# Regrouping the columns of a sparse matrix inside on-chip memory, in a graph layer followed by a mixture of experts

## The chip, the cores and the metric

The kernel runs on one core of a Trainium2 chip. The metric is device time in microseconds (us) of one execution. A core has five engines that run their own instruction streams and wait for each other by semaphores: TensorE (PE; its weight loads are PEld), VectorE (DVE), ScalarE (ACT), GpSimd (POOL) and SyncE (SP), which here only issues transfers. The transfers themselves are done by 16 DMA engines. On-chip memory (SBUF) has 128 rows, called partitions; matrix products land in a smaller memory, psum.

## The reference

A graph layer and a mixture of experts, one after the other, each with a residual:

```python
# x [2048, 256], src/dst [67584] with dst sorted, edge_weight [67584], node_vec1 [2048, 1]
xn = layernorm(x)
out = segment_sum(edge_weight[:, None] * xn[dst], src, 2048)   # edge_index = stack([src, dst])
x = x + out + node_vec1

xn = layernorm(x)
logits = xn @ Wr + br                  # 8 experts
top_p, top_idx = top_k(softmax(logits), 2)
weights = top_p / top_p.sum(-1)
for e in range(8):                     # hidden size 1024, exact gelu
    y[e] = gelu((layernorm(xn) * ln_g[e] + ln_b[e]) @ W1[e] + b1[e]) @ W2[e] + b2[e]
x = x + sum_k weights[:, k] * y[top_idx[:, k]]
```

The graph layer is a product A xn with a 2048 x 2048 matrix A that has an entry for each pair (src, dst) with edges, the sum of their weights.

## The kernel before

**Edge part.** The kernel makes A dense, block by block, and multiplies. A has 16 column blocks (a block is 128 values of dst) and 16 row blocks. The edges are sorted by dst, so two neighbouring columns ("a group") own a short window of edges. For each half of a column block (32 groups, 64 columns) `make_hots` (line 299) builds one-hot matrices of the edges: `hl` (line 306, VectorE) says which row within a row block, `eq` (line 311, VectorE) which row block and which of the two columns, and `hr` (line 318) is `eq` times the weight, split in three bfloat16 parts (two by VectorE, the third by GpSimd). `make_cols(n, ...)` (line 329) multiplies them on TensorE (line 343): 96 small products for a half block, n = 0 to 31, four groups at once in the four quarters of the array. The result in psum, `pa`, has 128 rows (4 groups x 2 columns x 16 row blocks, that is 8 columns of A times 16 row blocks) and, for four such m, 128 values each (the rows within a block). ScalarE copies it to `ar` (line 346, two copies for a half block; `ar` has three buffers).

The dense product wants a column of A in one partition: `ac` is [128 columns, 16 row blocks, 128]. So the 8 x 16 rows of `ar` have to become 8 rows with 16 pieces of 512 bytes each. Before the change this goes by way of memory: line 347 writes a half block to `ad` in memory (SP's queue, 512 KB), and after the second half line 350 reads the whole block back as `ac` (SP's queue, 1024 KB).

`dense(cbs, b)` (line 352) multiplies `ac` of a list of column blocks with the normalised rows `xn_sb` for two row blocks (line 357), and `add` (line 361) adds the result to `acc` on VectorE (lines 364 and 367). The column blocks come in groups of 3, 3, 3, 3 and 4 (`CS`, line 73); a group has 8 calls of `dense`, one for each pair of row blocks. `ac` tiles are in two rings, `cols_1` and `cols_0`, that the groups use in turn, with four buffers each; so a block of group g + 2 takes a buffer of group g, once that group's 8 calls are done.

The order is written by hand (manual schedule): step n issues the one-hots of n + 1, the additions of the calls of the step before, `make_cols(n)`, and then as many calls of `dense` as a budget allows (lines 500 to 507). The budget grows by 3.5 column blocks a step from n = 8 on; a call on three column blocks costs 3. In the last step, n = 31, all that is left of the first four groups is issued. The last group's calls follow after the branch at line 569, which is for inputs that the windows don't cover and isn't taken.

**Routing and experts.** The last group's calls alternate with the squares, the layer norm, the logits and the choice of two experts (lines 1088 to 1104). Rows are then sorted into slots of 256 of one expert, and each slot runs two layers on TensorE (lines 1013 and 1027). The weights of the first experts are asked for by SP (lines 932 to 935) right behind the last columns. SP's queue also carries, within the edge part, two blank blocks (lines 547 and 549) and small tables (line 540).

Of the kernel before, what the change touches and what calls it, by code (L numbers as in the profile page):

```python
# [9 lines left out]
F32 = mybir.dt.float32  # L10
# [11 lines left out]
P = 128  # L22
# [4 lines left out]
def kernel(  # L27
# [30 lines left out]
    nc = tc.nc  # L58
# [3 lines left out]
    NB = N // P  # L62
# [3 lines left out]
    GC = 2  # L66
# [3 lines left out]
    GB = P // GC  # L70
    GH = GB // 2
    QP = P // RK
# [15 lines left out]
    dram = ctx.enter_context(tc.tile_pool(name="dram", bufs=1, space=DRAM))  # L88
# [89 lines left out]
    pool_of = {cb: (cols_1, cols_0)[g % 2] for g, cbs in enumerate(groups) for cb in cbs}  # L178
# [150 lines left out]
    def make_cols(n, hl, hr):  # L329


        cb, h = n // 2, n % 2
        if h == 0:
            ads[cb] = dram.tile([P, NB, P], F32, name="ad", bufs=4)
        ad_v = ads[cb].rearrange("(m j) b r -> (j b) m r", m=GB // QP)
        ar = rowsp.tile([P, GH // QP, P], F32, name="ar")
        for m0 in range(0, GH // QP, 4):
            pa = ps_a.tile([P, 4, P], F32, name="pa")
            for m in range(4):
                for i in range(3):  # L340
                    for j in range(QP):
                        g = (m0 + m) * QP + j
                        nc.tensor.matmul(pa[j * RK:(j + 1) * RK, m, :], hr[:, i, g, :],  # L343
                                         hl[:, g, :], start=(i == 0), stop=(i == 2),
                                         tile_position=(0, j * RK))
            nc.scalar.copy(ar[:, m0:m0 + 4, :], pa)  # L346
        nc.sync.dma_start(ad_v[:, h * GH // QP:(h + 1) * GH // QP, :], ar)
        if h == 1:
            acs[cb] = pool_of[cb].tile([P, NB, P], F32, name="ac")
            nc.sync.dma_start(acs[cb], ads[cb])  # L350

    def dense(cbs, b):

# [14 lines left out]
                                           acc[:, b + i, :D], op0=OP.add, op1=OP.add)  # L368
        nc.vector.tensor_add(acc[:, b:b + 2, D:], acc[:, b:b + 2, D:], pa[:, :, D:DX])

    ads, acs = {}, {}
    ET = mybir.EngineType
    ALL = {ET.DVE, ET.Pool, ET.PE, ET.Activation, ET.SP}
    with tc.manual_schedule(engines=ALL):
# [88 lines left out]
        for n in range(NH):  # L463
# [3 lines left out]
            m = n % 4  # L467
# [26 lines left out]
            for p in late:  # L494
                add(*p)
            late = []
            make_cols(n, *hots.pop(n))


            if n >= 8:  # L500
                budget += 3.5
            while len(todo) > NB // 2 and (budget >= len(todo[0][0]) or n == NH - 1):
                cbs, b = todo.pop(0)
# [17 lines left out]
            if n == 1:  # L521
# [5 lines left out]
                for rows in (b1_rows, g_rows, be_rows, nv_rows):  # L527
                    m = rows.shape[0]
# [40 lines left out]
    with tc.If(n_used < E):  # L569
# [11 lines left out]
        with tc.tile_pool(name="any", bufs=2) as anyp, tc.tile_pool(  # L581
            name="ps_any", bufs=2, space=PSUM
# [594 lines left out]
    with tc.manual_schedule(engines=ALL - {ET.Pool}):  # L1177
        for q in range(4):
            r = slice(q * N // 4, (q + 1) * N // 4)
# [33 lines left out]
```

## Time and profile before

| | us |
|---|---|
| median of three runs | 506.23 |
| lowest and highest of them | 504.37, 507.13 |
| the profiled execution | 508.05 |
| its span, first to last instruction | 506.3 |
| TensorE busy | 459.8 (91%) |
| VectorE busy | 273.1 (54%) |
| GpSimd busy | 192.7 (38%) |
| ScalarE busy | 183.8 (36%) |

The profile's page gives, for one execution, the busy time of each engine, a picture of it in 40 slices, the DMA queues, the chain of work that ended last, the costliest groups of instructions, and the transfers by line with the median time from issue to landing. A group's line reads: source line, engine, operation, destination <- sources, count | busy us, mean ns of one | idle time of the engine before them and what ended most of it. A float32 product of the dense part appears as two records of its matmul. Other views of the same trace give the instructions in order of time, the waits, and the busy time of each engine in any stretch, with the clock that TensorE was granted (1.00 is full speed), the share of the DMA engines' time and GB/s.

### The profile page before, as it was taken

Reading aid. Unit: us, or ns where it says so; the run is one execution under the profiler, and the core shown is the slowest. Engines: PE = TensorE matmul, PEld = TensorE weight load, DVE = VectorE, ACT = ScalarE, POOL = GpSimd, SP = SyncE. Lnnn points to the kernel's source line nnn. Section 1 sums busy time; section 2 is a strip of 40 time slices with the busy share of each in tenths; the row PEclk is TensorE's granted clock in tenths of the full one; section 3 lists DMA queues with packets and bytes.
Section 4 is the critical chain, followed back from the end, with each engine's and each line's share of the span. In section 5 each row is a group of like instructions: output and inputs, shape, how many; then the busy total and the mean of one; then the engine's idle time right before and its main releaser. Section 6 shows DMA issues by size and latency. Waiting matters only on the chain.

```text
span 506.3 us, 12113 instructions
## 1 busy us (share of the span) xinstructions
PE 459.8 (91%) x4996; PEld 394.4 (78%) x4996; DVE 273.1 (54%) x621; ACT 183.8 (36%) x422; POOL 192.7 (38%) x158
## 2 busy tenths in 40 slices
PE   4876599898979999899999899999999999999993
PEld 3775478687758878788888788888888888888882
DVE  7999999999969971317837232323232312212111
ACT  2478524144214210028483323332243433333320
POOL 3477655544533330000142444443452444322231
PEclk9575679899979999999999999999999999999998
DMA  6128678796777667953513997997999677226420
GB/s 214 53 76 246 203 223 269 230 236 186 203 216 221 210 178 239 344 189 105 179 54 84 303 333 214 361 356 210 334 360 309 169 210 210 36 40 204 140 92 31
DMA packets 84356, 102.15 MB, mean 202 GB/s; under 512 B 8240, under 2 KB 74656, under 8 KB 82176
## 3 DMA queue, kind: packets, MB, share of 16 engines
q1 hardware_dynamic: 74832, 86.26, 53.5%
q0 software_dynamic: 7984, 13.91, 11.9%
q10 hardware_dynamic: 1472, 1.06, 0.7%
q8 instruction: 44, 0.72, 0.6%
q14 instruction: 24, 0.20, 0.1%
HBM read 75.18 MB, written 28.14 MB: 204 GB/s over the span
## 4 chain that ended last, share of the span: by engine, by line
PE 35%; DMA 13%; issue 3%; DVE 1%; SPq 0%; ACT 0%; POOL 0%; POOLq 0%; DVEq 0%
PE py L1027 16%; PE ph L1013 15%; DMA xs<-xr_d,to_i 8%; DMA y_d<-ys,to_i 2%; DMA out<-y_d 2%; PE px L978 1%; PE px L834 1%; PE py L357 1%; DMA so_far<-out,to_i 1%; DMA out<-ys,to_i 0%; SPq L1180 0%; POOL out L1048 0%; POOLq L1209 0%; ACT L1015 0%; DVE pick L957 0%
## 5 line engine op out<-in xcount | busy, mean ns | idle before, releaser
L357 PE MATMUL py<-xn_sb,ac 128*128 128x264 f32 x512 | 126.3, 404 | 1.8 <-DVEq L569 1.4
L1013 PE MATMUL ph<-xeT,w 128*128 128x256 f32 (+1 forms) x576 | 121.3, 368 | 2.4 <-PEq L1167 1.7
L1027 PE MATMUL py<-w,hT 128*128 128x256 f32 x544 | 121.0, 379 | 0.0
L1013 PEld LDWEIGHTS ph<-xeT,w 128*128 128x128 f32 x576 | 104.4, 190 | 16.5 <-issue 3.0
L357 PEld LDWEIGHTS py<-xn_sb,ac 128*128 128x128 f32 x512 | 98.5, 197 | 21.7 <-issue 2.2
L1027 PEld LDWEIGHTS py<-w,hT 128*128 128x128 f32 x544 | 101.9, 190 | 12.9
L1015 ACT ACTIVATE hT<-ph,ec 128x256 f32<-128x256 f32 (+1 forms) x144 | 66.2, 462 | 117.6 <-PE ph L1013 60.8
L1035 POOL DMA_INDIRECT y_d<-ys,to_i x30 | 48.5, 1616 | 119.3 <-DVE ys L1030 88.5
L318 POOL TENSOR_TENSOR hr<-eq,w 128x1024 bf16<-128x1024 bf16 x32 | 61.2, 1912 | 81.6 <-DVE hr L318 66.1
L343 PE MATMUL pa<-hl,hr 128*32 128x128 bf16 x3072 | 58.4, 237 | 21.6 <-POOL hr L318 10.8
L343 PEld LDWEIGHTS <-hr 128*32 128x32 bf16 x3072 | 50.0, 106 | 32.6 <-issue 14.0
L306 DVE TENSOR_TENSOR hl<-k,iota_t 128x4096 bf16<-128x4096 bf16 x32 | 72.9, 2278 | 0.0
L987 DVE TENSOR_SCALAR xeT<-px,ec 128x256 f32<-128x256 f32 (+1 forms) x38 | 18.4, 526 | 79.8 <-PE px L978 79.0
L939 POOL DMA_INDIRECT xs<-xr_d,to_i x39 | 40.5, 1038 | 54.2 <-DVE z L702 41.9
L346 ACT COPY ar<-pa 128x512 f32<-128x512 f32 x64 | 36.5, 584 | 59.8 <-PE pa L343 53.6
L1030 DVE SCALAR_TENSOR_TENSOR ys<-py,wt,b2w 128x256 f32<-128x256 f32 x34 | 16.4, 484 | 72.7 <-PE py L1027 61.3
L364 DVE TENSOR_TENSOR acc<-acc,py 128x528 f32<-128x528 f32 x32 | 22.3, 701 | 35.3 <-PE py L357 35.3
L318 DVE TENSOR_TENSOR hr<-eq,w 128x2048 bf16<-128x2048 bf16 x32 | 39.1, 1223 | 0.6
L1002 ACT ACTIVATE b2w<-b,wt 128x256 f32<-128x256 f32 x36 | 16.3, 500 | 34.0 <-DVE wt L1000 32.4
L311 DVE TENSOR_TENSOR eq<-k,iota_t 128x1024 bf16<-128x1024 bf16 x32 | 21.8, 680 | 0.0
L670 ACT ACTIVATE sq<-acc,less_m 128x256 f32<-128x256 f32 x16 | 8.0, 499 | 32.6 <-DVE acc L364 32.6
L296 ACT CAST w<-r 128x256 bf16<-128x256 f32 x16 | 6.5, 405 | 25.0 <-DVE r L295 25.0
(196 smaller groups left out, 303.0 us busy)
## 6 DMA issues: line engine op xcount, KB each, us to landing
w<-in_L_ffn_W SPq DMA_DIRECT2D x40, 1024.0 KB, 9.2
ad<-ar SPq DMA_DIRECT2D x32, 512.0 KB, 8.7
ac<-ad SPq DMA_DIRECT2D x16, 1024.0 KB, 5.9
b<-in_L_ffn_b SPq DMA_DIRECT2D x20, 128.0 KB, 9.8
out<-y_d SPq DMA_DIRECT2D x4, 512.0 KB, 6.3
xr_d<-rec SPq DMA_DIRECT2D x1, 1300.0 KB
y_d<-acc SPq DMA_DIRECT2D x1, 1280.0 KB, 5.1
acc<-in_x SPq DMA_DIRECT2D x2, 512.0 KB, 7.6
```

The source lines that it names most:

```text
L306: nc.vector.tensor_tensor(hl.rearrange("p g (n t) -> p g n t", t=2), two(k2[:, 0], g, P), pair(P), OP.is_equal)
L311: nc.vector.tensor_tensor(eq.rearrange("p g (n t) -> p g n t", t=2), two(k2[:, 1], g, RK), pair(RK), OP.is_equal)
L318: return engine.tensor_tensor(hr[:, i0:i1].rearrange("p i g (n t) -> p (i g) n t", t=2), eq[:, None, :, :].to_broadcast([P, i1 - i0, GH, RK]),
L343: nc.tensor.matmul(pa[j * RK:(j + 1) * RK, m, :], hr[:, i, g, :], hl[:, g, :], start=(i == 0), stop=(i == 2), tile_position=(0, j * RK))
L346: nc.scalar.copy(ar[:, m0:m0 + 4, :], pa)
L357: nc.tensor.matmul(pa[:, i, :DX], acs[c][:, b + i, :], xn_sb[:, c, :], start=(c == cbs[0]), stop=(c == cbs[-1]))
L364: nc.vector.tensor_add(acc[:, b:b + 2, :], acc[:, b:b + 2, :], pa[:, :, :DX])
L939: nc.gpsimd.indirect_dma_start(out=(sets[s.set][0] if into is None else into)[:, t, :], out_offset=None, in_=(xr_d if rows is None else ro ...
L1013: nc.tensor.matmul(ph, w1[:, k, c * P:(c + 1) * P], xeT[:, k, :], start=(k == 0), stop=(k == KD - 1))
L1015: nc.scalar.activation(hT[:, c, :s.n * P], ph, AF.Gelu, bias=ec[:, c:c + 1], scale=1.0)
L1027: nc.tensor.matmul(py, hT[:, c, t * P:(t + 1) * P], w2[:, c, :], start=(c == 0), stop=(c == KH - 1))
L1035: st = nc.gpsimd.indirect_dma_start(out=y_d[:, :], out_offset=bass.IndirectOffsetOnAxis(ap=tos[s.to][:, t:t + 1], axis=0), in_=ys, in_offs ...
```

## The change

`make_cols` no longer goes by way of memory. The tile `ac` is claimed in the first half of a column block instead of after the second, and behind each copy of line 346 SP issues four transfers of 64 KB, each from one m of `ar` (128 rows of 512 bytes) to 8 rows of `ac` (16 x 512 bytes each): 8 for a half block, 256 in all. The memory tile `ad` is gone. The budget of dense products grows from n = 7 on.

```diff
         cb, h = n // 2, n % 2
         if h == 0:
-            ads[cb] = dram.tile([P, NB, P], F32, name="ad", bufs=4)
-        ad_v = ads[cb].rearrange("(m j) b r -> (j b) m r", m=GB // QP)
+            acs[cb] = pool_of[cb].tile([P, NB, P], F32, name="ac")
         ar = rowsp.tile([P, GH // QP, P], F32, name="ar")
         for m0 in range(0, GH // QP, 4):
             pa = ps_a.tile([P, 4, P], F32, name="pa")
...
             nc.scalar.copy(ar[:, m0:m0 + 4, :], pa)
-        nc.sync.dma_start(ad_v[:, h * GH // QP:(h + 1) * GH // QP, :], ar)
-        if h == 1:
-            acs[cb] = pool_of[cb].tile([P, NB, P], F32, name="ac")
-            nc.sync.dma_start(acs[cb], ads[cb])
+            for m in range(m0, m0 + 4):
+                c = (h * GH // QP + m) * QP * GC
+                nc.sync.dma_start(acs[cb][c:c + QP * GC], ar[:, m, :])
...
-            if n >= 8:
+            if n >= 7:
                 budget += 3.5
```

More of the change, by code (lines that the diff above doesn't have):

```diff
@@ L369, in add @@
         nc.vector.tensor_add(acc[:, b:b + 2, D:], acc[:, b:b + 2, D:], pa[:, :, D:DX])
-    ads, acs = {}, {}
+    acs = {}
     ET = mybir.EngineType
```

## The prediction

> **What bounds the kernel now.** I read the page first. TensorE is busy for 459.8 us of 506.3, and the chain that ended last begins at 229.95 us and is mostly TensorE's own work, so whatever moves the end of the edge part moves the end of the kernel. Then I took the instructions in order of time around the end of the edge part, the starts of the one-hots (line 306), and the DMA queue's own waits.
>
> ```profile
> L357 PE MATMUL py<-xn_sb,ac 128*128 128x264 f32 x512 | 126.3, 404 | 1.8 <-DVEq L569 1.4
> ad<-ar SPq DMA_DIRECT2D x32, 512.0 KB, 8.7
> ac<-ad SPq DMA_DIRECT2D x16, 1024.0 KB, 5.9
> ```
>
> The first line (group, busy us, mean ns, idle before) says that the dense products are 512 records, and that none but 1.8 us of idle TensorE stands before them: the columns come late for nobody, and the trip through memory (8.7 us and then 5.9 us to landing) is hidden for 15 of the 16 column blocks. The last one is hidden too:
>
> ```profile
> 188.34 0.29 PE L343 MATMUL pa<-hl,hr 128*32 128x128 bf16 x8
> 190.42 1.41 PE L343 MATMUL pa<-hl,hr 128*32 128x128 bf16 x88 [1.78 <-POOLq L569]
> 191.26 1.21 ACT L346 COPY ar<-pa 128x512 f32<-128x512 f32 x2 [5.12 <-PE pa L343]
> 191.76 16.29 PE L357 MATMUL py<-xn_sb,ac 128*128 128x264 f32 x72
> ...
> 198.34 0.33 SPq L350 DMA_DIRECT2D ac<-ad  x1
> ...
> 209.45 25.16 PE L357 MATMUL py<-xn_sb,ac 128*128 128x264 f32 x112 [1.40 <-DVEq L569]
> ```
>
> Columns: start, duration, engine, line, records, idle time before and its releaser. The last half block's products end at 191.8 us. TensorE then works off what is left of the dense products, 72 records in 16.29 us, to 208.05 us. In that time the last columns land (198.34 + 5.9 = 204.2 us), 3.8 us before TensorE is free. So the path here is the backlog of dense products, not the columns. One call of dense() on three column blocks is 12 records, 12 x 16.29 / 72 = 2.72 us.
>
> ```profile
> 74.00:184.00 110.00, 102.88 (x2220) 83.67 (x2220) 99.99 (x129) 35.49 (x84) 48.11 (x30) 0.95 0.75 219
> L306 DVE TENSOR_TENSOR hl<-k,iota_t x32: 2253/2279/2286, 18.2 to 184.2; 128x4096 bf16<-128x4096 bf16 x32
> ```
>
> The stretch 74 to 184 us (busy us of TensorE, weight load, VectorE, ScalarE, GpSimd; granted clock, DMA share, GB/s) has TensorE at 94% and VectorE at 91%: two engines nearly full. The 32 one-hots start from 18.2 to 184.2 us, so a half block takes 166.0 / 31 = 5.35 us. That is the beat that the new transfers must keep.
>
> **The change, part by part.** *Dense one half block sooner.* The budget of 3.5 per half block starts at n = 7. The trace has 512 - 72 - 128 = 312 records before the backlog, 26 calls; with one more step the budget reaches 28 of the 32 calls, and the order of the built program shows that 4 are left after the last half block. The backlog shrinks from 72 records to 48, by 24 x 0.226 = 5.43 us. The two calls go elsewhere. One goes to n = 7, where TensorE waits for GpSimd's third factor twice (1.68 us before 59.83, 1.30 us before 63.88): 2.98 us of idle cover its 2.72 us, so it costs 0; without that cover 2.7 us. The first call today also waits for its columns (4 records at 66.35, the other 8 from 68.88 us); that could give back up to 1.8 us, of which I count nothing, since VectorE's beat comes next. The other call makes n = 30 a double one, ahead of the last half block, where TensorE today idles 1.78 us before 190.42: it costs 2.72 - 1.78 = 0.94 us. Its add on VectorE (0.70 us) falls into VectorE's 5.22 us of idle after 189.5 us, cost 0. Sum: -5.43 + 0.94 = **-4.5 us**.
>
> *The way through memory.* Removed: 32 transfers to memory and 16 back, and the wait of each second one for the first (102.9 us of waiting in SP's queue, which held up only later transfers). Added: 256 transfers of 64 KB (8 rows of 16 x 512 bytes), four behind each copy of line 346. Three things must each keep the beat, 5.35 / 8 = 0.67 us per transfer.
>
> ```profile
> L1180 SPq DMA_DIRECT2D out<-y_d x4: 576/594/1129, 474.8 to 477.3; - x4
> L350 SPq DMA_DIRECT2D ac<-ad x16: 332/333/338, 41.8 to 198.3; - x16
> 194.00:195.00 1.00, 1.00 (x7) 0.84 (x6) 0.26 (x1) 0.00 (x0) 0.00 (x0) 1.00 1.15 348
> ```
>
> (i) SP's issue: between 0.333 us and, in a row of four issued back to back, 0.594 us median and 1.129 us at most. I take 0.594 (the row of transfers issued back to back): 8 x 0.594 = 4.75 us of 5.35, it just fits. (ii) In flight: the built program has each transfer wait for the one eight places before it. Landings in the trace run from 4.0 us (8 KB, be_rows) to 8.7 us (512 KB); eight per landing is 0.50 to 1.09 us each. I take 4.0, since 64 KB is nearer to 8 KB than to 512: it fits. (iii) The movement itself. At 194 us only a transfer out of ar, in the same 512-byte pieces, is on the move: 348 GB/s with all 16 engines, or 0.19 us for 64 KB. If only as many engines work as there are destination rows, 8 of 16, it is 0.38 us. At the other end, if the rate goes with the rows written (348 GB/s over 128 rows, 2.7 GB/s a row), 8 rows take 21.75 GB/s, 3.0 us. No transfer in this trace writes so few rows with so many bytes. I take 0.38 us, from the row with the same source and the same pieces: 3.0 us of 5.35, hidden behind the one-hots.
>
> [...]
>
> New waits. The column tile is now claimed in the first half of its block instead of at the end, so its buffer must be free a half block sooner; dense() runs a half block sooner as well, and the program's order keeps only two transfers that wait for TensorE, where seven did (2.5 us of waiting in all). Behind such a one stand SP's next column transfers, and behind those ScalarE's copies once the three ar buffers are full, that is after two half blocks, 10.7 us: cost 0, and at most one call of 2.7 us if that cover is gone. ScalarE's copy into a reused ar waits for eight semaphores instead of one; today it waited for ad<-ar 5.3 us in three places, none of which TensorE's path shows, so 0. The small tables (line 540) hold SP's next transfer for 5.05 us today; that happens once more, behind the same three buffers: 0.
>
> The end of the edge part, now: TensorE's last products end near 192.7 us (191.76 + 0.94), the backlog of 4 calls takes 10.9 us, to 203.6. The last copy ends at 192.5 + 0.6; four issues (2.4 us) and the landing (6.3 us, out<-y_d, as a high value) give 201.8 us. So the columns are in 1.8 us before they are needed. The weights of the first expert follow on SP some 3 us sooner and land behind the columns; they are not read before 248 us. The 1.40 us at the branch (line 569) stays and is next, then the last group's products, all moved up together.
>
> Gaps of TensorE that no semaphore explains (0.42, 1.76, 1.44, 0.32, 3.06 us at 89 to 145 us) may shrink with less DMA traffic or grow with worse; I count 0, with 4 us to either side.
>
> Sum: 508.05 (profiled execution: span 506.3 and 1.75 around it) - 4.5 = 503.5. That execution lies 1.8 us over the median of the three runs, 506.23; against the median I predict **501.7 us** (506.23 - 4.5), by itself 497 to 503.5.
>
> **Rivals.** *A, few rows make it slow (slower than before).* The movement costs more than 0.67 us a transfer: from there on it sets the beat, ScalarE's copies wait for ar, TensorE for ScalarE's psum. With the middle (geometric) of 0.38 and 3.0, 1.07 us: 31.0 (first issue) + 256 x 1.07 + 6 (landing) = 311 us, against 209.45 for the start of the last group, so +101 us: 608 us. For it: 8 rows at a time, where every large transfer in the trace uses 128. Against it: four transfers behind one another go to different rows, and engines that run ahead of each other could use them at once; the DMA share of 0.75 falls, as half the bytes go. The outer end, 3.0 us, would be 31 + 768 + 6, +596 us, near 1,100.
>
> *B, the queue sets the beat.* Issue or the eight in flight take more than 0.67 us a transfer. With the 6.3 us landing of out<-y_d: 6.4 / 8 = 0.80 us, 31 + 205 + 6 = 242 us, +32: 539 us. For it: 0.594 leaves 11% of room, and VectorE's short steps (4.7 us) leave none. Against it: the early and the double steps are longer, and three ar buffers even it out.
>
> *C, nothing to gain.* The columns were hidden before and TensorE at 94% just does the calls elsewhere: what the backlog loses, the edge part gains, and only the idle found at n = 30 and n = 7 remains, 2 us or less, perhaps lost to a longer clock drop (the granted clock is 0.5 at 144 to 149 us already). 505 us. The change would then do what it says and not matter.
>
> **How the numbers follow.** 0.5% of 506.2 is 2.5 us, about what a measurement of this kernel can tell from no change. Forecast (hidden, backlog shorter): 0.40. A: 0.33, a quarter of it above 640. B: 0.15. C: 0.12, of which 0.10 within 0.5% and 0.02 slower. Faster 0.40, same 0.10, slower 0.50: the likeliest single case is the fast one, though the slow ones together outweigh it. The range runs from 498 (under it 0.05) to 640, which takes in B, the middle of A and most of what lies above it; left out are 0.08 above and the outer end of the movement's price.
>
> **What will show it.** Right: 48 records of line 357 (the dense products) in one block after the last half block, no wait of ScalarE's copies for the transfers, one-hots still at 5.35 us a half block, the last group starting near 204 us. A: copies that wait for the column transfers in each half block, one-hots 8 us or more apart, TensorE's granted clock no excuse. B: SP's queue full of issues, or waiting for the transfer eight before, with little DMA share. C: the steps at n = 7 and n = 30 longer by a call. What would make it wrong above all is step (iii), the price of writing 64 KB into 8 rows.

## The result, and the profile after

The changed kernel takes 525.11 us (median of four executions, 515.78 to 532.27) against 506.68 us of the kernel before (504.37 to 508.92). The ratio is 1.0285, with a 95% interval of 1.0215 to 1.0354: slower, where 501.7 us was predicted. The ratio and its interval leave out executions more than 1.5% above the fastest of their kernel (here 527.25 and 532.27 us), the medians do not. The profiled execution is the fastest of the four: 515.78 us, span 513.8, that is 7.5 us over the span of before. The execution profiled before is one of its longer ones (508.05 us, where the median of the 35 recorded in all is 504.64), so 7.5 us is rather too little. The trace below explains most of these 7.5 us and not the rest of the spread.

On the page of the changed kernel, the group of dense products, the copy to `ar` (line 345 now), and the transfers:

```profile
L355 PE MATMUL py<-xn_sb,ac 128*128 128x264 f32 x512 | 129.0, 408 | 7.3 <-DMA ec<-cols_d 4.2
L345 ACT COPY ar<-pa 128x512 f32<-128x512 f32 x64 | 35.3, 586 | 79.2 <-DMA ac<-ar 60.3
ac<-ar SPq DMA_DIRECT2D x256, 64.0 KB
```

TensorE now stands idle for 7.3 us ahead of the dense products; it was 1.8 before the change. The second line is the new one: ScalarE waits 60.3 us for column transfers, because all three `ar` buffers are still being read. A wait of ScalarE alone need cost nothing (before the change it stood 59.8 us ahead of the same copies); the instructions of SP's queue in order of time (start, duration, line, count) show what lies behind it:

```profile
29.59 51.12 SPq L348 DMA_DIRECT2D ac<-ar  x72
80.82 0.43 SPq L545 DMA_DIRECT2D xr_d<-none  x1
81.29 0.46 SPq L547 DMA_DIRECT2D y_d<-none  x1
81.85 21.64 SPq L348 DMA_DIRECT2D ac<-ar  x32
103.60 0.41 SPq L538 DMA_DIRECT2D cols_d<-by_e  x1
104.10 106.86 SPq L348 DMA_DIRECT2D ac<-ar  x152
213.16 0.37 SPq L930 DMA_DIRECT2D ec<-cols_d  x1
```

From 29.6 to 211 us SP issues column transfers almost without a pause; three other transfers stand between them. The tile view of `ac` gives the durations of the 256 issues (min, median, max in ns) and the starts of the first and the last:

```profile
L348 SPq DMA_DIRECT2D ac<-ar x256: 604/613/1441, 29.6 to 210.3; - x128
```

From one start to the next it is (210.3 - 29.6) / 255 = 0.709 us on average. In the undisturbed stretches it is 0.672 (eight transfers in 5.38 us; 0.613 of issue and 0.059 until the next one starts), and no eight take less. The other 9.4 us (255 x 0.037) are a dozen stretched issues of up to 1.44 us (5.0 us over the usual ones), the three other transfers (1.7 us), one wait for ScalarE's copy near 36 us (1.4 us) and small gaps. The beat allows 0.669. The difference, 0.040 x 255, is 10.2 us, and by so much the last column transfers come late. At 0.672 alone it would be 0.8 us: the issue takes all the room that the beat has, and whatever comes on top is never made up. TensorE, in order of time at the two ends of the edge part:

```profile
63.07 2.13 PE L355 MATMUL py<-xn_sb,ac 128*128 128x264 f32 x4
66.44 3.86 PE L355 MATMUL py<-xn_sb,ac 128*128 128x264 f32 x8 [1.24 <-DMA ac<-ar]
...
196.36 10.95 PE L355 MATMUL py<-xn_sb,ac 128*128 128x264 f32 x48
208.70 1.57 PE L355 MATMUL py<-xn_sb,ac 128*128 128x264 f32 x6 [1.40 <-DMA ac<-ar]
214.52 26.22 PE L355 MATMUL py<-xn_sb,ac 128*128 128x264 f32 x106 [4.24 <-DMA ec<-cols_d]
```

The backlog has the 48 records that were forecast, but it starts at 196.36, not 192.7, and then the last columns are missing: after six records TensorE stands 4.24 us and goes on at 214.52. Before the change the seventh record of this group came at 210.8 us (209.45 + 6 x 25.16 / 112), so that is 3.7 us late. The name ec<-cols_d there is that of the transfer issued right behind the columns; the packet records have the last 512-byte piece of a column at 213.4 us, just before TensorE goes on.

The rest of the group is slower as well: 106 records in 26.22 us, where 106 took 23.8 us at the pace of before. The granted clock is the last figure but two in these windows, of the kernel before and of the changed one:

```profile
209.00:235.00 26.00, 25.43 (x120) 21.50 (x121) 8.97 (x27) 10.41 (x32) 0.00 (x0) 1.00 0.66 224
```

```profile
214.00:241.00 27.00, 26.22 (x106) 21.73 (x106) 7.83 (x23) 10.27 (x31) 0.00 (x0) 0.90 0.88 297
```

So 6.1 of the 7.5 us are there at the end of this block: 3.7 of standing and 2.4 of slower products at a granted clock of 0.90 instead of 1.00.

### The profile page after: what moved, and what is told of

The parts are those of the page before. It is cut to its first block, busy times and chain, and to the rows that moved or that the text cites. A ratio compares the mean times of both kernels' runs of the same rounds, so it can differ in the third digit from the quotient of the medians.

```text
span 513.8 us, 12518 instructions
## 1 busy us (share of the span) xinstructions
PE 467.0 (91%) x4996; PEld 396.9 (77%) x4996; DVE 273.0 (53%) x621; ACT 182.5 (36%) x422; POOL 192.8 (38%) x158
## 4 chain that ended last, share of the span: by engine, by line
PE 38%; DMA 13%; issue 4%; DVE 1%; ACT 1%; SPq 0%; POOL 0%; POOLq 0%; DVEq 0%; ACTq 0%
PE py L1025 16%; PE ph L1011 15%; DMA xs<-xr_d,to_i 7%; PE py L355 4%; DMA y_d<-ys,to_i 2%; DMA w<-in_L_ffn_W 2%; DMA out<-y_d 1%; PE px L976 1%; PE px L832 1%; DMA so_far<-out,to_i 1%; DMA out<-ys,to_i 0%; SPq L1178 0%; POOL out L1046 0%; DMA ec<-cols_d 0%; DVE acc L362 0%
## 5 line engine op out<-in xcount | busy, mean ns | idle before, releaser
L355 PE MATMUL py<-xn_sb,ac 128*128 128x264 f32 x512 | 129.0, 408 | 7.3 <-DMA ec<-cols_d 4.2
L1011 PE MATMUL ph<-xeT,w 128*128 128x256 f32 (+1 forms) x576 | 123.0, 372 | 2.7 <-PEq L1165 2.0
L1011 PEld LDWEIGHTS ph<-xeT,w 128*128 128x128 f32 x576 | 105.5, 192 | 17.5 <-issue 3.3
L342 PE MATMUL pa<-hl,hr 128*32 128x128 bf16 x3072 | 59.5, 233 | 18.3 <-POOL hr L318 10.6
L345 ACT COPY ar<-pa 128x512 f32<-128x512 f32 x64 | 35.3, 586 | 79.2 <-DMA ac<-ar 60.3
L408 PEld LDWEIGHTS pa<-wc,ar 128*128 128x128 f32 x64 | 11.2, 272 | 3.5 <-ACT ar L402 3.1
```

Source lines behind the costliest of these rows:

```text
L355: nc.tensor.matmul(pa[:, i, :DX], acs[c][:, b + i, :], xn_sb[:, c, :], start=(c == cbs[0]), stop=(c == cbs[-1]))
L1011: nc.tensor.matmul(ph, w1[:, k, c * P:(c + 1) * P], xeT[:, k, :], start=(k == 0), stop=(k == KD - 1))
```

## The experiments

**Theory T**: the number of issues is the price. SP cannot issue column transfers closer than 0.672 us on average, and that is the beat's whole allowance. **Rival M** (later **P**): moving 64 KB into 8 rows is the price. **Rival F**: the eight transfers in flight are. Line numbers in the fences are those of each kernel, a few off from the changed one.

### Issue from two engines

```diff
-                nc.sync.dma_start(acs[cb][c:c + QP * GC], ar[:, m, :])
+                (nc.sync, nc.scalar)[m % 2].dma_start(acs[cb][c:c + QP * GC], ar[:, m, :])
```

> The same 256 transfers, issued in turn by SP and by ScalarE. Theory (SP's issue sets the beat: 0.672 us from one issue to the next, 5.38 us for the eight of a half block, and 12.7 us behind ScalarE's last copy at the end): SP has 128 issues, 2.7 us a half block, the last columns land near 197 us, TensorE does not wait for them, time 499 to 504 us. Rival M (moving 64 KB into 8 rows sets the beat, issue only waits behind it): the movement is the same, last columns near 210 us, time 514 to 526. Rival F (eight in flight sets the beat): as M, since the eight are shared.

Measured: 563.67 us (558.34 to 575.46), ratio 1.1113 (1.0968 to 1.1258). T's number is missed by 60 us. ScalarE's waits, by line (total us, times, longest):

```profile
ACT ar L345 <- DMA ac<-ar: 55.0, 20, 5.5
ACT w L296 <- DMA ac<-ar: 14.8, 6, 3.6
ACT k L281 <- DMA ac<-ar: 12.2, 5, 4.1
```

With the issues on ScalarE's own stream its other work (lines 296 and 281, which feed VectorE's one-hots) stands behind transfers too. And one transfer still takes 0.88 us on average (256 from 30.4 to 253.8), though two queues issue: with half of the issues taken from SP, something else sets the spacing. SP now waits for it, 60.5 us for the transfer eight before against 0.3 us in the changed kernel. The packet records point at the movement: a 512-byte piece takes 60 ns on average here (30 to 255 us), 43 in the changed kernel (30 to 212 us). Why it is slower from two queues is not shown. So T is not the whole of it: taking half of the issues from SP brought nothing here (ratio 1.1113, where the changed kernel has 1.0285). They went to an engine with work of its own, at 0.624 us each (median; 0.613 on SP).

### The same number of transfers, into all rows

```diff
-                c = (h * GH // QP + m) * QP * GC
-                nc.sync.dma_start(acs[cb][c:c + QP * GC], ar[:, m, :])
+                nc.sync.dma_start(acs[cb][:, h * GH // QP + m, :], ar[:, m, :])
```

and the same bytes in a quarter of the transfers:

```diff
+            u = h * GH // QP + m0
+            nc.sync.dma_start(acs[cb][:, u:u + 4, :], ar[:, m0:m0 + 4, :])
```

> 256 transfers of 64 KB from SP as in the changed kernel, in the same 512-byte pieces, but each into all 128 rows of the column tile (one piece a row) instead of 8 rows; the columns then stand in the wrong places, so the graph layer multiplies with another matrix of the same shape. Theory (issue): nothing gets better, issues 0.67 us apart, last columns near 210 us, 512 to 525 us; only the issues that are stretched beyond 0.61 us may go (7 us in all, at most). Rival M: the movement falls to some 0.2 us a transfer, SP is no longer held, and the time falls to 500 to 504 us.

> As rows_128 (columns in the wrong places), but the four transfers behind a copy are one of 256 KB: the same bytes and pieces in 64 issues instead of 256. Theory (issue): SP has two issues a half block, the last columns land within 4 us of the last copy, 499 to 504 us. Rival M: no difference to rows_128. Rival F: faster than rows_128 as well, since fewer are in flight; the spacing of the issues in rows_128 tells it from the theory.

Measured: 545.01 us (541.6 to 546.84) and 522.52 us (520.41 to 523.77). The columns lie in wrong places, the routing differs and more expert slots run (5146 matmuls instead of 4996 in the first), so only the edge part is compared. The issues, and TensorE at the end of the edge part, first of the 256 transfers, then of the 64:

```profile
L347 SPq DMA_DIRECT2D ac<-ar x256: 464/599/1985, 30.1 to 223.0; - x128
```

```profile
204.94 10.95 PE L354 MATMUL py<-xn_sb,ac 128*128 128x264 f32 x48
217.30 7.36 PE L354 MATMUL py<-xn_sb,ac 128*128 128x264 f32 x32 [1.41 <-DVEq L566]
```

```profile
186.20 10.95 PE L354 MATMUL py<-xn_sb,ac 128*128 128x264 f32 x48
198.54 25.16 PE L354 MATMUL py<-xn_sb,ac 128*128 128x264 f32 x112 [1.39 <-DVEq L566]
```

Into 128 rows 256 transfers are no faster than into 8 (0.756 us from start to start, last group at 217.30), although they move fast: a 512-byte piece takes 27 ns, and SP never waits for the transfer eight before. T had expected 0.67 us and fewer stretched issues, and missed that: 27 of them cost 23 us over the usual issue, where the changed kernel has a dozen and 5.0 us. A quarter of the issues, with the same bytes and the same 512-byte pieces, brings the last group to 198.54, 18.8 us sooner and 10.9 sooner than the kernel before (the shorter backlog is in the 10.9). That is T: where nothing but the number of issues, and with it the size of each, changes, the delay goes. M is refuted as the cause of the floor, and F with it.

### The way on chip alone

```diff
-            if n >= 7:
+            if n >= 8:
```

> The on-chip transfers alone, dense products from n = 8 as before. Theory (issue): the last columns still land near 213 us; the longer backlog (72 records, 16.3 us) ends near 211, so it fills time in which TensorE waits in the changed kernel: the same as the changed kernel within 3 us, 513 to 526. If the second part did cost something by itself (a longer step at n = 7 and n = 30, buffers claimed too soon), this is faster than the changed kernel by 3 us or more; if buffers of the column tiles hold SP back, it is slower by 3 us or more.

Measured: 530.48 us (519.9 to 543.36), over the 513 to 526 expected, and profiled in its longest execution, so the total tells nothing finer than "as slow as both parts together". SP also waits 5.6 us there for column buffers that TensorE still reads (nothing in the changed kernel); what that costs cannot be told from this spread. The windows of the long execution (TensorE, weight load, VectorE, ScalarE, GpSimd busy; clock, DMA share, GB/s):

```profile
74.00:150.00 76.00, 68.15 (x1453) 54.94 (x1455) 67.01 (x96) 23.56 (x61) 35.77 (x24) 0.96 0.57 117
158.00:190.00 32.00, 24.13 (x497) 19.08 (x496) 25.28 (x24) 4.90 (x10) 10.19 (x6) 0.95 0.65 71
```

From 158 us on the DMA engines are busier and move less: 71 GB/s at a share of 0.65, 109 GB/s to a full share, against 205 before that. There the issues still take 0.613 us, but SP waits between them and eight transfers take 7.7 us instead of 5.38, 0.96 us each. The clock is no excuse (0.96 and 0.95). That is M's mechanism, in part of the time. That it is what makes this execution longer than others is not shown, since no shorter one of this kernel was profiled.

### The order of the rows

All eight transfers of a half block behind its second copy, once so that neighbours in the queue go to rows 32 apart, once in plain order (range(8) in place of the list) as a control:

```diff
-            for m in range(m0, m0 + 4):
-                c = (h * GH // QP + m) * QP * GC
-                nc.sync.dma_start(acs[cb][c:c + QP * GC], ar[:, m, :])
+        for m in (0, 4, 1, 5, 2, 6, 3, 7):
+            c = (h * GH // QP + m) * QP * GC
+            nc.sync.dma_start(acs[cb][c:c + QP * GC], ar[:, m, :])
```

Rival P takes the place of the rows for the price: with neighbours 32 rows apart, a transfer should cost 0.97 us or more in all of the edge part (the author's estimate; 0.96 was measured in the slow stretch of chip_from_8).

> All eight transfers of a half block are issued behind its second copy, in the order m = 0, 4, 1, 5, 2, 6, 3, 7, so that neighbours in the queue go to rows 32 apart (rows 0-7, then 32-39, then 8-15 and so on). The same is computed. Theory T (SP's issue, 0.672 us from one transfer to the next, is the floor, and where the rows lie does not matter): 0.67 us a transfer as in the changed kernel, last group at 214 to 218 us, total 515 to 532. [...]

> The control of same_ports: all eight transfers behind the second copy, but in the order m = 0 to 7, as the changed kernel has them. The same is computed. Both theories: like the changed kernel, 0.67 us a transfer in most stretches, last group 214 to 218 us, total 515 to 532 (1 to 2 us more at the end, as the last eight wait for the second copy). If this one is as slow as same_ports, the order of the rows says nothing.

Measured: 532.18 us (527.96 to 535.32), ratio 1.0505 (1.0441 to 1.0570), against 517.09 (514.39 to 519.6), ratio 1.0243 (1.0193 to 1.0292) for the control. SP's column transfers and its waits for the transfer eight before, rows 32 apart first:

```profile
30.08 69.58 SPq L348 DMA_DIRECT2D ac<-ar  x72
...
124.25 107.70 SPq L348 DMA_DIRECT2D ac<-ar  x152
```

```profile
SPq L348 <- DMA ac<-ar: 18.3, 34, 1.4
```

and the control:

```profile
30.23 52.22 SPq L348 DMA_DIRECT2D ac<-ar  x72
...
106.12 106.91 SPq L348 DMA_DIRECT2D ac<-ar  x152
```

```profile
SPq L348 <- DMA ac<-ar: 1.3, 3, 0.7
```

The order of the rows costs 15 us, with the same issues of the same bytes: place matters, and T's "where the rows lie does not matter" is wrong. But it costs only in the first 72 transfers (0.97 us each against 0.73); the last 152 take the same time in both, so P's 0.97 us in all of the edge part is wrong as well. Within the 72 it goes higher, rows 32 apart first, then the control:

```profile
43.92 21.36 SPq L348 DMA_DIRECT2D ac<-ar  x19
```

```profile
43.81 21.47 SPq L348 DMA_DIRECT2D ac<-ar  x32
```

In the same time 19 transfers go out instead of 32, 1.12 us each against 0.67. Two limits lie side by side: the issue, 0.67 us at best for transfers into 8 rows; and the movement, which is usually hidden behind it and in some stretches takes 0.96 to 1.16 us (1.16 for the slowest sixteen in a row here). Why rows 32 apart are the slower order, and why a stretch of slow movement begins and ends, is open.

### The dense products sooner, without the transfers on chip

The way through memory, budget from n = 7:

```diff
-            if n >= 8:
+            if n >= 7:
                 budget += 3.5
```

> The way through memory of the kernel before, and the dense products one half block sooner. The same is computed. If the second part of the change is worth what the prediction gave it (backlog 72 to 48 records, -5.4 us, n = 30 +0.9): 501.7, ratio 0.991. Theory T: the gain is real only where the columns are there; the call at n = 7 waits for column block 2, which through memory lands near 69 us, so TensorE stands still for some 3 to 5 us more there and gives most of it back: 504 to 507, ratio 0.997 to 1.002.

Measured: 507.21 us (505.68 to 509.18), before 505.39, ratio 1.0036 (1.0010 to 1.0061). TensorE at n = 7 and behind the last half block:

```profile
62.78 2.13 PE L357 MATMUL py<-xn_sb,ac 128*128 128x264 f32 x4
69.76 3.75 PE L357 MATMUL py<-xn_sb,ac 128*128 128x264 f32 x8 [4.85 <-DMA ac<-ad]
...
196.23 12.56 PE L357 MATMUL py<-xn_sb,ac 128*128 128x264 f32 x48 [2.28 <-issue]
210.19 25.16 PE L357 MATMUL py<-xn_sb,ac 128*128 128x264 f32 x112 [1.40 <-DVEq L569]
```

The call stands 4.85 us for column block 2, as T had it, and there is no gain (if anything, 0.4% slower). That the one makes the other is not shown by this trace: the last half block's products end near 194 us, only 1 us later than in the next kernel, and 3.9 us more go at the backlog, in an idle that no semaphore explains (2.28) and in slower records (12.56 us instead of 10.95; the granted clock is 0.91 from 192 to 210 us). With a larger step instead of an earlier start, as many calls leave the backlog, and the first comes at n = 8 as in the kernel before:

```diff
             if n >= 8:
-                budget += 3.5
+                budget += 3.75
```

> The kernel before with a budget of 3.75 instead of 3.5 column blocks a step from n = 8: the columns go through memory, no call comes before its columns, and two calls more are done before the last half block, as in the changed kernel (backlog 48 records). The same is computed. T: 72 to 48 records is -5.4 us, +0.9 at the end, last group near 204 to 206, total 501 to 503, ratio 0.991 to 0.995. V: the last half block's products come 3 us or more later than 190.4, last group at 207 to 210, ratio 0.998 to 1.004.

Measured: 503.05 us (499.54 to 507.59), before 504.64, ratio 0.9943 (0.9906 to 0.9981): faster than both kernels, than the one before by little.

```profile
65.27 1.16 PE L357 MATMUL py<-xn_sb,ac 128*128 128x264 f32 x4
70.50 3.46 PE L357 MATMUL py<-xn_sb,ac 128*128 128x264 f32 x8 [4.08 <-DMA ac<-ad]
...
191.73 1.41 PE L343 MATMUL pa<-hl,hr 128*32 128x128 bf16 x88 [0.55 <-POOLq L569]
193.08 10.95 PE L357 MATMUL py<-xn_sb,ac 128*128 128x264 f32 x48
205.42 25.16 PE L357 MATMUL py<-xn_sb,ac 128*128 128x264 f32 x112 [1.40 <-DVEq L569]
```

In this execution the first call waits as well, 4.08 us, and yet the time is made up by the end of the edge part, which speaks further against the wait at n = 7 as the whole cause above. The last half block's products come 1.3 us later than before (190.42), the backlog has 48 records, the last group starts 4.0 us sooner. So in this form the shorter backlog is worth something: -2.9 us measured (504.64 x 0.0057; by the interval -1.0 to -4.7), where -4.5 us was forecast for the form with the earlier start.

### A few blocks on chip

Column blocks 2 and 15 on chip, the others through memory, budget from n = 7; then blocks 0, 1, 2 and 15; `(2, 15)` becomes `(0, 1, 2, 15)`:

```diff
-            acs[cb] = pool_of[cb].tile([P, NB, P], F32, name="ac")
+            if cb in (2, 15):
+                acs[cb] = pool_of[cb].tile([P, NB, P], F32, name="ac")
+            else:
+                ads[cb] = dram.tile([P, NB, P], F32, name="ad", bufs=4)
...
+        if cb in (2, 15):
+            return
+        ad_v = ads[cb].rearrange("(m j) b r -> (j b) m r", m=GB // QP)
+        nc.sync.dma_start(ad_v[:, h * GH // QP:(h + 1) * GH // QP, :], ar)
...
```

> Only column blocks 2 and 15 go by transfers on chip (32 instead of 256), the other 14 through memory; dense products one half block sooner. The same is computed. Theory T (the issues cost, not the way itself): a burst of 16 transfers per block, 0.67 us each, is 10.8 us in 10.7 us of two half blocks and leaves no queue behind; the call at n = 7 has its columns in time, the last columns land near 200 us, before the backlog of 48 records ends: last group near 204 to 206, total 501 to 504, ratio 0.990 to 0.996. Rival P (movement into few rows sets the beat everywhere): 32 transfers at 0.97 us or more, 15.5 us per block, the columns of block 2 some 5 us late and those of block 15 near 205: 505 to 509, ratio 0.998 to 1.005.

> Column blocks 0, 1, 2 and 15 go by transfers on chip (64 in all), the other 12 through memory; dense products one half block sooner. The same is computed. In two_blocks the first call at n = 7 stood 6.0 us for column block 2, whose transfers sat in SP's queue behind the read of block 1. Theory T (the issues are the price; the second part of the change is worth its 4.5 us where the columns are there): the first call waits 1.3 us or less, the last group starts near 204 to 206, total 501 to 504, ratio 0.991 to 0.997. Rival V (VectorE sets the pace of the edge part at 98% from 74 to 130 us, the calls done sooner push the end of the edge part back by what they take off the backlog): one-hots end at 186 us or later, last group at 207 to 210, 505 to 508, ratio 0.998 to 1.004.

Measured: 506.75 us (503.33 to 511.78), before 505.39, ratio 1.0025 (0.9987 to 1.0063); and 505.33 us (502.24 to 513.8), before 504.64, ratio 1.0004 (0.9969 to 1.0040). Both miss T's totals and lie in those of the rivals, P (505 to 509) and V (505 to 508). TensorE at n = 7 and at the last group, first with two blocks, then with four:

```profile
61.81 1.16 PE L366 MATMUL py<-xn_sb,ac 128*128 128x264 f32 x4
68.95 3.56 PE L366 MATMUL py<-xn_sb,ac 128*128 128x264 f32 x8 [5.98 <-DMA ad<-ar]
...
208.09 25.16 PE L366 MATMUL py<-xn_sb,ac 128*128 128x264 f32 x112 [1.40 <-DMA w<-in_L_ffn_W]
```

```profile
66.67 1.66 PE L366 MATMUL py<-xn_sb,ac 128*128 128x264 f32 x4
69.11 2.02 PE L366 MATMUL py<-xn_sb,ac 128*128 128x264 f32 x8 [0.78 <-DMA ac<-ar]
...
205.50 25.16 PE L366 MATMUL py<-xn_sb,ac 128*128 128x264 f32 x112 [1.40 <-DVEq L578]
```

With two blocks, block 2 comes no sooner than through memory: SP issues its first transfer at 52.7 us, after the read of block 1, and the 16 take 13.0 us, between T's 10.8 and P's 15.5. With four, the wait is 0.78 us and the last group starts at 205.50, as T said and not V (207 to 210); that profiled execution, 502.24 us, is the fastest of its twelve, and the others take it back. What they spend it on was not traced: inconclusive, and V is not refuted for them.

Two more, built on rate_375's edit with block 15 alone on chip, the second with a step of 4:

> As rate_375, with column block 15 alone on chip (16 transfers). The same is computed. Through memory the last columns land near 204 us, just when a backlog of 48 records ends; on chip a copy at 192 us and 8 issues of 0.67 us with a landing of 2 to 3 us give 200 to 201. T: equal to rate_375 or up to 1 us better, ratio 0.989 to 0.995. V: 0.998 to 1.004.

> A budget of 4 column blocks a step from n = 8 (backlog 24 records), with column block 15 alone on chip. The same is computed. T: another 2 calls out of the backlog, 5.4 us, against 2 x 2.9 us of TensorE's time in an edge part with 6.9 us of idle from 74 to 184 us, of which rate_375 uses most: equal to rate_375_last within 2 us, and the columns of block 15 then come just as the backlog ends; ratio 0.988 to 0.997. V: slower, the end of the edge part pushed back by more than the backlog loses, ratio 1.000 to 1.010.

Measured: 503.37 us (500.81 to 511.32), ratio 0.9972 (0.9942 to 1.0003), not to be told from rate_375 and not from the kernel before; and 506.45 (502.39 to 509.68), ratio 1.0014 (0.9977 to 1.0051). With the step of 4 only 24 records are left, and the columns are late: TensorE stands 5.78 us in the last group and goes on with its seventh record at 209.63, only 1.2 us sooner than before (210.8). The movement shows here too: the last eight of the 16 transfers start 0.93 us apart, the first eight 0.69. More out of the backlog than the columns' landing allows is not a gain.

## Why the prediction was wrong, point by point

- **Step (i), SP's issue, failed.** It took 0.594 us for an issue and compared 8 x 0.594 = 4.75 us with a beat of 5.35. Measured: 0.613 us of issue, 0.059 to the next, and 0.037 for stretched issues and what else stands in the queue, 0.709 on average, 5.67 us for eight. The duration was 3% off; the error was to take a duration where the beat needs the time from start to start. The row quoted for it had that time too: four issues from 474.8 to 477.3 us are 2.5 / 3 = 0.83 us apart. With that number the step would not have fit. It is rival B's mechanism, priced there at 0.80 us and 539 us, measured at 0.709 and 525. The prediction named step (iii) as the one that would make it wrong; it was this one. Rows_128_four, where the same bytes go in a quarter of the issues, shows it.
- **Step (ii), eight in flight,** held in the changed kernel: 0.3 us of waiting. Rival F falls as a cause there; where SP does wait so, in two_queues, chip_from_8 and same_ports (60.5, 23.6 and 18.3 us), the count is the place where slow movement shows.
- **Step (iii), the movement,** taken at 0.38 us, is not what set the floor. For most of the time it stays hidden behind the issues, so the runs bound it there at 0.67 us; where it shows, 0.38 was too low: 0.96 to 1.16 us, about the 1.07 of rival A. A's sign, copies that wait for the column transfers, came too, but a queue full of issues makes them wait as well: the sign did not tell A from B. That it makes the executions of the changed kernel differ (515.78 to 532.27) is likely by chip_from_8's windows, but not shown: no trace of a longer execution of the changed kernel exists. The 640 us in A's chance and at the upper end of the range are shown by no run or trace: the changed kernel took 515.78 to 532.27 us, and the slowest form that was run, two_queues, at most 575.46.
- **New waits at cost 0** failed with (i). The cover named was three `ar` buffers, 10.7 us of slack; with a queue that never catches up they fill once and stay full, and ScalarE waits 60.3 us.
- **Columns in by 201.8 us**: the last issue starts at 210.3 and TensorE goes on at 214.52. The weights of the first experts, issued from 213.16 on, cost little: TensorE's one stall for them is 1.23 us near 293 us, and at the same place it stood 1.88 us before, for another transfer.
- **Backlog 72 to 48 records** came as forecast, with 10.95 us for it, and so did the double call at n = 30 (+1.3 us in rate_375, +0.94 forecast). The call at n = 7 cost little in the changed kernel (a wait of 1.24 us; 4.85 in memory_from_7, where the columns come through memory). Why that kernel gains nothing and rate_375 does stays open.
- **Rival C**, nothing to gain (2 us or less): in the form of rate_375 a gain is measured, but its interval (1.0 to 4.7 us) takes in C's 2 us; in the form of the earlier start, with columns in time for most of it (four_blocks), no gain could be measured, so for that form it stands.
- **The granted clock** has no term in the sum. It is not the cause of the lag (0.959 in the profiled execution after, 0.945 before), but the 2.4 us of slower products in the last group go with a clock of 0.90. It is 0.89 to 0.93 there in the five traced kernels whose last group stands for its columns (the changed one, chip_from_8, same_ports, late_in_order, rate_4_last) and 1.00 in six where it does not (before, memory_from_7, rate_375, rate_375_last, two_blocks, four_blocks). The pace agrees: after the stand 106 records take 26.22, 25.51, 25.51 and 25.24 us (the changed kernel, same_ports, late_in_order, rate_4_last), where the pace of the six, 112 in 25.16 us, gives 23.8.

Of the 7.5 us in the span, 6.1 lie ahead of the end of the last group's main part (240.7 us). The rest, 1.4 us, lies behind it and was not taken apart.

## What to carry to other kernels

A transfer that was hidden is not made cheaper by making it shorter: here one of 512 KB became eight of 64 KB, the bytes fell by half, and the price became the number of issues. When many small transfers must keep a beat, compare the time from one issue's start to the next, with the longest of the row in the mean, and leave room: at 0.709 us against 0.669 a lag of 10 us builds up in 255 steps, and since the queue itself is behind, more buffers would not bring the last columns sooner (not tried). Rows_128_four shows what fewer issues are worth: the same bytes in a quarter of them bring the last group 18.8 us sooner than in rows_128. Before a change of two parts is kept or dropped, run each alone: here the smaller part, in another form (a step of 3.75), was the only gain.

## What was not expected of the hardware

- The time of an issue on SP goes with the transfer's form more than with its size in these traces: medians of 0.333 us (1 MB read back into `ac`), 0.426 (512 KB from `ar` to memory), 0.466 (256 KB into 128 rows, rows_128_four), 0.599 (64 KB into 128 rows in a full queue, rows_128; 0.464 at least) and 0.613 (64 KB into 8 rows). Single issues stretch to 1.44 us, and in rows_128 to 1.99; what stretches them is open.
- Movement into 8 rows had two speeds for the same transfers in one execution: 205 and 109 GB/s for a full DMA share in two windows of chip_from_8. The packet records of the traces say the same of a single 512-byte piece: 27 ns into 128 rows (rows_128; from 130 to 190 us 91 GB/s at a share of 0.32), means of 37 to 62 ns in the changed kernel by stretches of 10 us (101 GB/s at 0.52 from 130 to 170 us), 69 to 79 from 30 to 80 us with rows 32 apart (same_ports; 84 GB/s at 0.67 from 32 to 80 us).
- In the traces a last group that stands 2.3 to 8.7 us for its columns is followed by products at a granted clock of 0.89 to 0.93; without the stand it is 1.00. That one makes the other was not tested.
